# Products of the identity in the planned gaps of the matmul engine, a branch whose idle side follows in line, and a new order, in a planned four-stage block

## The chip, the cores and the metric

The kernel runs on one core of a Trainium2 chip. The metric is the device time of one execution in microseconds (us): the median of several runs. One further execution was taken with the hardware profiler; its span runs from the first to the last instruction.

## What is computed

The input `x` is 32 sequences of 256 tokens with 128 channels, float32. Four residual steps follow one another, each behind a layer normalisation:

```python
x = x + attn_a(layernorm(x), ...)   # delta-rule recurrence over 256 steps, 128 x 128 state, gated
x = x + ffn(layernorm(x), w_gate, w_up, w_down)    # silu(x @ wg.T) * (x @ wu.T) @ wd.T, hidden 384
x = x + attn_b(layernorm(x), ...)   # in-projection, causal convolution of 4 taps, silu,
                                    # state-space scan in chunks (4 heads of 64), gate, norm, out-projection
x = x + ffn(layernorm(x), w_gate, w_up, w_down)    # the same weights again
```

The recurrence of `attn_a` is, per token, `S = S @ (a * (I - b * k k^T)) + b * v k^T` and `o = (q @ S) * gate`. The weights of `ffn` come as integers in -127..127 and are scaled by 1/127.

## The kernel before

**Tiling.** Two sequences make a unit: 512 tokens, four tiles of 128. There are 16 units, and `units()` writes down for each, in turn, `attention` (stage 0), `ffn` (stage 1), `ssd` (stage 2) and `ffn` (stage 3), with a load of `x` ahead and a store of the result behind. In `attention` the recurrence is a blocked triangular inverse: VectorE inverts blocks of 16 by forward substitution (tiles `rows_a`, `u_a`, `step_a`), after their elements went through DRAM (`blocks_a`), and the matmul engine doubles the blocks from 16 to 128 (`pt_a`, `p_a`, with copies `t_a` on ScalarE between, and `pair` for the last level). In `ffn` the products are `fg`, `fu` and `fy`; in `ssd` they are `pz`, `pc` (the convolution's input, read by VectorE into `cy_s`), `pl`, `cb_ps`, `sy_ps`, `pf`, `gT_ps` and `so`. `norm_t` makes the transposed normalised input, `xT_ps`, for every stage.

**The planner.** None of the helpers (`matmul`, `transpose`, `act`, `vec`, `pool`, `dma`) emits anything: each adds an `Op` with an engine, a cost in ns (`busy`), a latency (`late`) and its predecessors, worked out from the parts of buffers that it reads and writes. Matmuls are recorded at line 238, transposes at 251, ScalarE at 259 and 261, VectorE at 275, GpSimd at 292, DMAs at 302, whatever they compute. `Planner.run` then makes a list schedule of all operations of all units over PE, DVE, ACT, POOL and SP: at each step it takes, of the operations that could start within 20 ns of the earliest on their engine, the one with the lowest key. The key is `at(unit)`, that is a multiple of `period` plus a `SHIFT` for each unit (with the last three units drawn together by `LAST`), plus the length of the unit's remaining path, plus a `STAGE` for each of the four stages. It is raised by `SWITCH` for an activation function whose table is not loaded, and by `KEEP` for a change between full products and 64-column pieces (`op.cut`, the `sy_ps` pieces). The plan's start times sort the operations, and in that order they are emitted; each engine executes its own in order. The plan's times themselves are used for nothing else.

**Buffers.** Every buffer takes one of a fixed number of slots of its kind (`SLOTS`); kind `ps` is the eight PSUM banks. A bank is claimed when its first product is placed, no earlier than `EARLY` ns ahead of the time at which everything that the bank's products need from outside (`gate`) is done. An operation on the chip waits for its operands and, where it is the first to write a slot, for the last reader of the buffer that had the slot before it.

**The branch.** A product of the float32 pair form (`exact`) serves where the weights are small integers. At line 1203 every engine loads the flag `large`; at line 1204 a `tc.If(large > 0)` holds a second program of the whole computation with full weights, planned and emitted anew. With these inputs the flag is 0, and every engine jumps over it to the kernel's end.

Constants that the change touches are at lines 153 to 166, `add` at 203, `gates` at 312, `run` from 333, the identity `ident` at 509, the branch at 1204.

Of the kernel before, what the change touches and what calls it, by code (L numbers as in the profile page):

```python
# [18 lines left out]
P = 128  # L19
# [128 lines left out]
class Planner:  # L148
# [2 lines left out]


    SLOTS = {"ps": 8, "m": 56, "l": 10, "t": 12, "s": 64, "d": 6, "g": 6, "b": 3, "e": 4}
    SWITCH = 76800.0
    HOP, SLACK = 30.0, 130.0
    STAGE = (0.0, -8900.0, 1900.0, 0.0)
    EARLY = 0.0
    SPARE = {"ps": 0.5, "m": 3, "l": 0.5, "t": 1, "s": 2, "d": 0.5, "g": 0.5, "b": 0.5, "e": 0.5}
    LAST = 0.12
    SHIFT = (18900.0, -4200.0, 0.0, 0.0, 1500.0, 11400.0, 1600.0, 1500.0, 0.0, 0.0, 19300.0, -27800.0, -1400.0, -9200.0, -7200.0, -5400.0)  # L160
    HALF = "be"
    RATE = 270.0
    LANES = 8
    CUT = 150.0
    KEEP = 3900.0
    SIZES = {"ps": 512, "m": 512, "l": 1024, "t": 64, "s": 32, "d": 512, "g": 8192, "b": 384, "e": 12288}

    def __init__(self, tc, pools, period, window):
# [34 lines left out]
    def add(self, eng, busy, late, emit, outs, ins, table=None, after=(), lock=False):  # L203
        op = Op()
        op.eng, op.busy, op.late, op.emit, op.table, op.lock = eng, busy, late, emit, table, lock
        op.unit, op.n, op.stage = self.unit, len(self.ops), self.stage
        op.preds, op.succs, op.bufs = {p.n: p for p in after}, [], []
        op.moves, op.cut, op.batch = 0.0, 0, ()
        for v, write in [(v, False) for v in ins] + [(v, True) for v in outs]:
            if not isinstance(v, View):  # L210
                continue
            bits = v.bits()
            for other, obits, lanes, owrite in v.buf.seen:
                if (
                    other is not op and (write or owrite) and bits & obits
                    and lanes[0] < v.lanes[1] and v.lanes[0] < lanes[1]
                ):
                    op.preds[other.n] = other
            kept = v.buf.kind == "c" and not v.buf.again
            assert self.setup or not (kept and write)  # L220
            if self.setup or not kept:
                v.buf.seen.append((op, bits, v.lanes, write))
            if v.buf.kind == "c" and v.buf.tile is None:
                v.buf.tile = self.pools["c"].tile(list(v.buf.dims), v.buf.dtype, tag=v.buf.name, name=v.buf.name)
            if v.buf.kind != "c" and v.buf not in op.bufs:
                op.bufs.append(v.buf)
        for p in op.preds.values():
            p.succs.append(op)
        self.ops.append(op)
        return op  # L230
# [42 lines left out]
    def vec(self, name, out, *args, ins=(), more=0, n=None, rate=0.96, **kw):  # L273
        def emit():
            getattr(self.tc.nc.vector, name)(real(out), *map(real, args), **{k: real(v) for k, v in kw.items()})  # L275

        busy = (_count(out) if n is None else n) / rate + 65 + more

        data = {"tensor_tensor": 2, "tensor_tensor_scan": 2, "scalar_tensor_tensor": 3, "tensor_scalar": 1}.get(name, 0)
        data = [v for i, v in enumerate(args[:data]) if (name, i) != ("scalar_tensor_tensor", 1)]  # L280
        lock = bool(data) and not any(isinstance(v, View) and v.buf.kind == "ps" for v in data)
        self.add("DVE", busy, 85, emit, [out], list(args) + list(kw.values()) + list(ins), lock=lock)

    def pool(self, name, out, *args, ins=(), cost=None, **kw):
        n = _count(out)
        if cost is None:
            cost = {
                "tensor_tensor": 1.66 * n + 149, "tensor_scalar": n + 260, "tensor_copy": n + 190, "memset": 0.97 * n + 60,
            }.get(name, n / 2 + 100)

        def emit():
            getattr(self.tc.nc.gpsimd, name)(real(out), *map(real, args), **{k: real(v) for k, v in kw.items()})  # L292

        lock = name == "tensor_tensor" and n > NT
        self.add("POOL", cost, 40, emit, [out], list(args) + list(kw.values()) + list(ins), lock=lock)
# [16 lines left out]
    def gates(self):  # L312
# [7 lines left out]
        for b, ops in users.items():  # L320
# [4 lines left out]
                    of.add(self.ops[n])  # L325
            b.gate = {p for op in ops for p in op.preds.values()} - of

    def at(self, unit):

        late = max(0, unit - (self.units - 3))  # L330
        return (unit - late + late * self.LAST) * self.period + self.SHIFT[unit]

    def run(self):
# [9 lines left out]
        for op in ops:  # L343
            op.key = (self.at(op.unit) + longest[op.unit] - op.tail + self.STAGE[op.stage], op.n)
            op.wait, op.ready, op.placed = len(op.preds), 0.0, False
# [6 lines left out]
        free = dict.fromkeys(engines, 0.0)  # L352
# [9 lines left out]
        order = []  # L362
        while len(order) < len(ops):
            best = None
            for e in engines:
                rest = []
                for op in cands[e] if e != "PE" or not rest_of else rest_of:
# [6 lines left out]
                    for b in op.bufs:  # L374
                        if b.slot is None:
# [5 lines left out]
                            if b.kind == "ps":  # L381
                                if not all(p.placed for p in b.gate):
                                    ok = False
                                    break
                                t = max([t] + [p.done - self.EARLY for p in b.gate])
                    if ok:
# [5 lines left out]
                if e == "ACT" and table is not None:  # L392
                    same = [
                        ((k[0] + (self.SWITCH if op.table and table not in op.table else 0), k[1]), t, op)
                        for k, t, op in same
                    ]
                if e == "PE":
                    same = [((k[0] + (self.KEEP if op.cut != cut else 0), k[1]), t, op) for k, t, op in same]
                pick = min(same, key=lambda x: x[0])
# [3 lines left out]
            t, op = best  # L403
# [35 lines left out]
                oldest += 1  # L439
        self.span = max(op.done for op in ops)  # L440
        order.sort(key=lambda op: (op.start, op.n))
        with self.tc.manual_schedule():
            for op in order:
                for b in op.bufs:
                    if b.tile is None:
                        size = self.SIZES[b.kind]
                        flat = self.pools[b.kind].tile([1 if b.kind in "dge" else P, size], BF16 if b.kind in self.HALF else F32, tag=f"{b.kind}{b.slot[1]}", name=b.name + self.mark)
                        b.tile = flat[:, : b.size]
                        if len(b.dims) > 2:
                            names = " ".join(f"d{i}" for i in range(1, len(b.dims)))  # L450
                            b.tile = b.tile.rearrange(
                                f"p ({names}) -> p {names}", **{f"d{i}": b.dims[i] for i in range(2, len(b.dims))}
                            )
                op.emit()


# [5 lines left out]
def hybrid_block(ctx: ExitStack, tc: tile.TileContext, ins: dict, out: bass.AP):  # L462
# [36 lines left out]
    pl = Planner(tc, pools, period=17900.0, window=6)  # L499
# [6 lines left out]
            pattern=pattern, channel_multiplier=by,  # L506
        )

    ident = pl.const([P, P], "ident")
    pool("memset", ident, 0.0)  # L510
    select(ident, ALU.not_equal, 0, [[-1, P]], 1, fill=1.0)

# [124 lines left out]
    def whole(name, src):  # L637
        wi = pl.buf("m", [P, NF, P], f"wi_{name}").bitcast(I32)
        pl.dma(wi, src, late=3600)
        wf = pl.buf("m", [P, NF, P], f"wf_{name}")  # L640
        vec("tensor_copy", wf, wi)
        return wf

    def turned(name, wf):
        pt = pl.buf("ps", [P, NF, P], f"wt_{name}")
        for f in range(NF):
            pl.transpose(pt[:, f, :], wf[:, f, :], ident)
        return pt
# [15 lines left out]
    large = pl.const([P, 1], "large", I32)  # L664
# [516 lines left out]
    def units():  # L1181
        pl.setup = False
        for g in range(n_units):
            pl.unit = g
            rows_of = slice(g * SEQS, (g + 1) * SEQS)
            x0 = big([P, NT, P], f"x0_{g}")
            pl.dma(x0, x_in[rows_of].rearrange("s (c p) d -> p (s c) d", p=P))
            pl.stage = 0
            x1 = attention(g, x0)
            pl.stage = 1  # L1190
            x2 = ffn(g, x1, "f", "x2")
            pl.stage = 2
            x3 = ssd(g, x2)
            pl.stage = 3
            x4 = ffn(g, x3, "h", "x4")
            pl.dma(out[rows_of].rearrange("s (c p) d -> p (s c) d", p=P), x4)
        pl.run()
# [3 lines left out]


    large = nc.values_load(large.real()[0:1, 0:1], min_val=0, max_val=P)
    with tc.If(large > 0):
        exact, (w_gate, w_up) = False, full
        pl.restart()
        pl.mark = "_full"
        for name, dst, src in (("gate_full", w_gate, gate_src), ("up_full", w_up, up_src)):
            vec("tensor_copy", dst, turned(name, whole(name, src)))
        units()  # L1210
# [34 lines left out]
```

## Time and profile before

| | us |
|---|---|
| median of 3 runs | 805.45 |
| lowest and highest | 802.44, 805.91 |
| the profiled execution | 806.73 |
| its span | 804.9 |
| PE busy, instructions | 744.7, 5485 |
| DVE busy, instructions | 684.3, 2386 |
| ACT busy, instructions | 597.2, 1443 |
| POOL busy, instructions | 364.0, 597 |
| mean granted clock of TensorE | 0.975 |

PE is the matmul engine (TensorE), PEld its weight loads, DVE VectorE, ACT ScalarE, POOL GpSimd, SP SyncE. The busy time of PE includes each product's way through the array, so that neighbours overlap and a busy PE is not a full one. `PEclk` and "granted clock" are the share of TensorE's full clock that the chip grants. A float32 product is two records in the trace. The names of tiles are those of the program with the unit's number left out, so `p_a` stands for all products of that name in `attention`. A wait is named after what ended last before it, which can be an operand or the last reader of a buffer's previous content.

### The profile page before, as it was taken

Reading aid. Unit: us, or ns where it says so; the run is one execution under the profiler, and the core shown is the slowest. Engines: PE = TensorE matmul, PEld = TensorE weight load, DVE = VectorE, ACT = ScalarE, POOL = GpSimd, SP = SyncE. Lnnn points to the kernel's source line nnn. Section 1 sums busy time; section 2 is a strip of 40 time slices with the busy share of each in tenths; the row PEclk is TensorE's granted clock in tenths of the full one; section 3 lists DMA queues with packets and bytes.
Section 4 is the critical chain, followed back from the end, with each engine's and each line's share of the span. In section 5 each row is a group of like instructions: output and inputs, shape, how many; then the busy total and the mean of one; then the engine's idle time right before and its main releaser. Section 6 shows DMA issues by size and latency. Waiting matters only on the chain.

```text
span 804.9 us, 16786 instructions
## 1 busy us (share of the span) xinstructions
PE 744.7 (93%) x5485; PEld 616.5 (77%) x5485; DVE 684.3 (85%) x2386; ACT 597.2 (74%) x1443; POOL 364.0 (45%) x597
## 2 busy tenths in 40 slices
PE   5958999899999999999999999899999999998886
PEld 4646886687878888877988878686789988776775
DVE  4794799989988889889999689989898778999964
ACT  5833467979687877779787798897955578997862
POOL 8994332262452815514732634646631123243550
PEclk9976999999999999999999999999999999999999
DMA  5221110010110002101011002011201000000001
GB/s 145 82 68 42 29 42 1 5 33 1 56 30 24 22 7 67 42 27 33 18 30 31 27 15 58 16 45 44 67 4 43 14 5 1 5 15 5 13 10 44
DMA packets 42159, 25.48 MB, mean 32 GB/s; under 512 B 18448, under 2 KB 37840, under 8 KB 42064
## 3 DMA queue, kind: packets, MB, share of 16 engines
q1 hardware_dynamic: 41056, 24.13, 11.1%
q8 instruction: 45, 0.74, 0.4%
q14 instruction: 50, 0.41, 0.2%
q10 hardware_dynamic: 1008, 0.20, 0.1%
HBM read 19.16 MB, written 5.14 MB: 30 GB/s over the span
## 4 chain that ended last, share of the span: by engine, by line
PE 52%; DVE 20%; ACT 15%; POOL 5%; issue 3%; DMA 2%; SPq 1%; ACTq 0%; DVEq 0%; POOLq 0%
PE p_a L238 6%; PE fy_f L238 5%; DVE cy_s L275 4%; PE fy_h L238 4%; PE fg_f L238 3%; ACT L261 3%; PE sy_ps_s L238 3%; PE so_s L238 2%; PE fu_f L238 2%; PE pc_s L238 2%; PE fg_h L238 2%; PE fu_h L238 2%; PE pt_a L251 2%; DVE u_a L275 2%; PE cb_ps_s L238 2%
## 5 line engine op out<-in xcount | busy, mean ns | idle before, releaser
L275 DVE SCALAR_TENSOR_TENSOR cy_s<-pc_s,cw,cy_s 128x510 f32<-128x510 f32 (+2 forms) x192 | 137.6, 731 | 2.9 <-ACT cy_s L261 2.3
L261 ACT ACT_TABLE_LOAD x66 | 84.7, 1283 | 9.9 <-DMA x<-in_L_attn_a_x_dram 5.8
L238 PE MATMUL fy_f<-wdT,hT_f 128*128 128x128 f32 x384 | 74.5, 280 | 0.0
L238 PE MATMUL fy_h<-wdT,hT_h 128*128 128x128 f32 x384 | 72.1, 281 | 0.6 <-DVE hT_h L275 0.3
L238 PEld LDWEIGHTS fy_f<-wdT,hT_f 128*128 128x128 f32 x384 | 61.4, 191 | 6.3 <-issue 3.6
L238 PE MATMUL pc_s<-xT_s,w_xbc 128*128 128x512 f32 x128 | 64.5, 599 | 1.3 <-ACT gT_s L259 0.7
L238 PEld LDWEIGHTS fy_h<-wdT,hT_h 128*128 128x128 f32 x384 | 59.1, 191 | 8.1 <-issue 4.3
L275 DVE TENSOR_TENSOR step_a<-rows_a,u_a 128x16 f32<-128x16 f32 (+14 forms) x240 | 51.7, 216 | 7.5 <-DMA rows_a<-blocks_a 3.1
L275 DVE TENSOR_TENSOR u_a<-u_a,step_a 128x16 f32<-128x16 f32 (+14 forms) x240 | 54.3, 227 | 3.9
L261 ACT ACTIVATE cy_s<-pc_s,cb,cw 128x512 f32<-128x512 f32 x64 | 48.3, 779 | 9.3 <-PE pc_s L238 9.1
L292 POOL TENSOR_TENSOR xd_s<-xt_s,dt_s 128x512 f32<-128x512 f32 x32 | 33.2, 1045 | 42.9 <-ACT xt_s L259 42.2
L238 PE MATMUL so_s<-w_out,gT_s 128*128 128x128 f32 x256 | 45.8, 290 | 1.9 <-DVE cy_s L275 1.2
L238 PEld LDWEIGHTS so_s<-w_out,gT_s 128*128 128x128 f32 x256 | 39.7, 204 | 6.6 <-ACT cy_s L261 1.4
L261 ACT ACTIVATE sc_s<-cy_s 128x512 f32<-128x512 f32 x64 | 38.9, 636 | 3.6 <-DVE cy_s L275 1.9
L275 DVE SCALAR_TENSOR_TENSOR sm_s<-pl_s,cb_s 128x512 f32<-128x512 f32 x64 | 41.3, 680 | 0.3 <-ACT pl_s L261 0.2
L292 POOL TENSOR_TENSOR sy_s<-sy_s,yo_s 128x256 f32<-128x256 f32 x32 | 24.6, 773 | 35.5 <-DVE sy_s L275 14.2
L238 PEld LDWEIGHTS p_a<-t_a,neg_a 128*128 128x128 f32 x256 | 36.4, 203 | 5.5 <-ACT t_a L259 3.7
L238 PE MATMUL p_a<-t_a,neg_a 128*128 128x64 f32 x256 | 38.1, 280 | 1.8 <-DVE x L275 1.3
L238 PEld LDWEIGHTS p_a<-x_a,t_a 128*128 128x128 f32 x256 | 36.6, 201 | 3.7 <-ACT t_a L259 2.3
L238 PE MATMUL p_a<-x_a,t_a 128*128 128x64 f32 x256 | 37.9, 274 | 1.0 <-ACT t_a L259 1.0
L259 ACT COPY t_a<-pt_a 128x256 f32<-128x256 f32 (+1 forms) x64 | 20.2, 316 | 24.0 <-PE pt_a L251 22.9
L275 DVE TENSOR_TENSOR hT_f<-fth_f,fu_f 128x512 f32<-128x512 f32 x48 | 31.2, 681 | 7.3 <-PE fu_f L238 4.8
(253 smaller groups left out, 2420.7 us busy)
## 6 DMA issues: line engine op xcount, KB each, us to landing
rows_a<-blocks_a SPq DMA_DIRECT2D x128, 64.0 KB
x<-in_L_attn_a_x_dram SPq DMA_DIRECT2D x16, 256.0 KB
dec_a<-row_a SPq DMA_DIRECT2D x16, 256.0 KB
out_dram<-x SPq DMA_DIRECT2D x16, 256.0 KB
blocks_a<-neg_a SPq DMA_DIRECT2D x128, 4.0 KB
cuts_s<-cut_s SPq DMA_DIRECT2D x48, 8.0 KB
sums_t<-cuts_s SPq DMA_DIRECT2D x32, 12.0 KB
sums_s<-cuts_s SPq DMA_DIRECT2D x16, 24.0 KB
```

What stands on the lines that cost most here:

```text
L238: self.tc.nc.tensor.matmul(real(out), lhsT=real(lhsT), rhs=real(rhs), start=start, stop=stop)
L251: self.tc.nc.tensor.transpose(real(out), real(in_), real(ident))
L259: self.tc.nc.scalar.copy(real(out), real(in_))
L261: self.tc.nc.scalar.activation(real(out), real(in_), func, bias=real(bias), scale=real(scale), **kw)
L275: getattr(self.tc.nc.vector, name)(real(out), *map(real, args), **{k: real(v) for k, v in kw.items()})
L292: getattr(self.tc.nc.gpsimd, name)(real(out), *map(real, args), **{k: real(v) for k, v in kw.items()})
```

## The change

It has three parts. A new method `keep_busy` walks the plan's PE operations in order of start and looks at the gap between the end of one and the start of the next (`free` begins at 1700 ns). If the gap is over `IDLE` (300 ns), if no PE operation has yet written the bank's buffer and if the operation is not a 64-column piece, it notes `int(gap * 0.7 / 223)` fillers. These are emitted just ahead of the operation: products of the identity with itself, 128 columns, float32, into the first columns of the operation's own bank, which the operation then overwrites. Nothing reads them, and the plan is made without them.

The branch gets `preferred_fallthrough_block=False`, which asks that the side not taken by `large > 0` follow in line.

Seven numbers of the planner are changed, which give a new order of all operations on all engines.

```diff
-    SWITCH = 76800.0
+    SWITCH = 46100.0
     HOP, SLACK = 30.0, 130.0
-    STAGE = (0.0, -8900.0, 1900.0, 0.0)
-    EARLY = 0.0
+    STAGE = (0.0, -7600.0, 1900.0, 0.0)
+    EARLY = 300.0
...
-    LAST = 0.12
-    SHIFT = (18900.0, -4200.0, 0.0, 0.0, 1500.0, 11400.0, 1600.0, 1500.0, 0.0, 0.0, 19300.0, -27800.0, -1400.0, -9200.0, -7200.0, -5400.0)
+    LAST = 0.1
+    SHIFT = (18900.0, -4200.0, 0.0, 0.0, 1500.0, 11400.0, 1600.0, 1500.0, 0.0, 0.0, 6700.0, -27800.0, -1400.0, -9200.0, -7200.0, -6000.0)
...
-    KEEP = 3900.0
+    IDLE, WARM = 300.0, 0.7
+    KEEP = 3100.0
...
+    def keep_busy(self, order):
+
+
+        written, free = set(), 1700.0
+        for op in order:
+            if op.eng != "PE":
+                continue
+            bank = next(b for b in op.bufs if b.kind == "ps")
+            gap = op.start - free
+            if gap > self.IDLE and bank not in written and not op.cut:
+                op.warm, op.bank = int(gap * self.WARM / 223), bank
+            written.add(bank)
+            free = op.start + op.busy
...
         order.sort(key=lambda op: (op.start, op.n))
+        self.keep_busy(order)
...
+                for _ in range(op.warm):
+                    n = min(P, op.bank.size)
+                    one = self.ident.real()
+                    self.tc.nc.tensor.matmul(op.bank.flat[:, :n], lhsT=one, rhs=one[:, :n], start=True, stop=True)
                 op.emit()
...
-    ident = pl.const([P, P], "ident")
+    ident = pl.ident = pl.const([P, P], "ident")
...
-    with tc.If(large > 0):
+    with tc.If(large > 0, preferred_fallthrough_block=False):
```

## The prediction

> **What bounds the kernel now.** I read the page first, then the matmul engine's clock record and busy time by stage, then the chain of waits inside the slow stages, then the matmul engine's waits, then the last microseconds.
>
> The page:
>
> ```profile
> span 804.9 us, 16786 instructions
> ...
> PE 744.7 (93%) x5485; PEld 616.5 (77%) x5485; DVE 684.3 (85%) x2386; ACT 597.2 (74%) x1443; POOL 364.0 (45%) x597
> ...
> PEclk9976999999999999999999999999999999999999
> ...
> PE 52%; DVE 20%; ACT 15%; POOL 5%; issue 3%; DMA 2%; SPq 1%; ACTq 0%; DVEq 0%; POOLq 0%
> ```
>
> The matmul engine (PE) is the nearest to full and holds 52% of the chain. How full it really is comes from the start-to-start times of its records where it runs without a stop: a 128-column float32 product is two records of about 111 ns, a 512-column one two of 430 ns. Pricing every record so gives 677 us of work at full clock. Walking the records in order, each starting when the one before has taken its price, leaves 102 us of real gaps, 60 us of them in 69 gaps longer than 0.3 us; the remaining 20 us to the last product (798.5 us) is work at half clock. So there are three pots: 677 fixed, 102 of gaps, 20 of cold clock.
>
> The clock record has 0.5 in 47.90-58.14, 64.96-78.62, 242.46-245.87, 730.56-733.98, 754.46-757.87, 771.52-774.94 and from 802.24 on. Before 17.18 us it has no entry, and the "1.00" that windows print there is empty: two 512-column products take 2.05 us at 12.7 us and 1.02 us at 21.2 us, so the start is cold too. By stage (length, then busy time of PE, PEld, DVE, ACT, POOL, granted clock, DMA):
>
> ```profile
> 42.00:54.00 12.00, 3.57 (x15) 1.97 (x14) 11.15 (x37) 4.38 (x10) 11.59 (x21) 0.75 0.38 111
> ...
> 59.00:65.00 6.00, 4.13 (x21) 2.49 (x19) 5.79 (x24) 2.52 (x12) 1.22 (x7) 1.00 0.02 2
> 65.00:79.00 14.00, 12.70 (x58) 11.67 (x58) 4.12 (x16) 3.68 (x11) 8.53 (x11) 0.51 0.22 59
> ...
> 140.00:700.00 560.00, 540.41 (x4135) 454.28 (x4135) 497.02 (x1734) 443.36 (x1054) 237.28 (x372) 1.00 0.10 28
> ```
>
> From 42 to 54 VectorE and GpSimd are full and PE idles; from 65 to 79 only PE is full, and at half clock. The chain there (start, us), against the same products later at full clock:
>
> ```profile
> 64.96 1.98 PE p_a L238 x8
> ...
> 67.39 1.99 PE p_a L238 x8
> ...
> 69.95 1.11 PE pt_a L251 x4
> 71.06 0.64 PE kT_ps_a L251 x3
> 71.70 1.86 PE p_a L238 x8
> ...
> 74.01 1.97 PE p_a L238 x8
> 75.98 1.71 PE pt_a L251 x8
> 77.69 1.58 PE p_a L238 x10
> ```
>
> ```profile
> 102.69 0.84 PE p_a L238 x8
> ...
> 113.72 0.22 PE fy_f L238 x2
> ```
>
> Eight p_a records cost 1.98 us cold and 0.84 us warm. Last, line 1204, the branch:
>
> ```profile
> L1204 SPq EVENT_SEMAPHORE  x8: 17/17/17, 803.0 to 803.5; - x8
> ...
> L1204 SPq COMPARE_BRANCH  x1: 53/53/53, 799.8 to 799.8; - x1
> ```
>
> SyncE branches at 799.85 and executes its next instruction at 802.98: 3.1 us of nothing. The last output bytes land at 801.81.
>
> **What the Trainium skill says.** "TensorE: Matmul & The Clock Gate", section "What's actually happening": the array's clock is cut to half by default and after an idle window, given back after a busy one, in windows of 3413 ns. The trace agrees on the steps: four cold entries are 3.41 us, the others 10.24 and 13.65, three and four of them. The same page, "HAM oscillation": gaps over about 3.4 us recool it. Here the trace is stricter: from 65 to 79 gaps of 0.4 to 0.7 us kept it cold for four windows, and it warmed after solid work (75.8 to 78.6). "Runtime: NRT & Kernel Launch", "Instruction fetch mechanics": a taken branch out of the fetched pages waits for a fetch by DMA; the 3.1 us after the branch, with two instruction packets of 0.42 to 1.29 us inside, fit. "ScalarE: Activation LUTs", "What ACT_TABLE_LOAD costs": 1283 ns a load; the page shows 66 with mean 1283.
>
> **The change part by part**, against the profiled execution's own 806.73 us (span 804.9 and 1.83 around it); it lies 1.28 above the median of the three runs, 805.45, and I carry that over.
>
> *The branch.* If the side with no work follows in line, SyncE goes on at 799.95: its eight semaphore steps (0.6 us) lie beside the last output's landing at 801.81, after which its waits (up to 0.46 us) and the closing 0.78 us remain: end at about 803.1 for 804.9. VectorE's own jump (799.35 to 802.27) goes as well. -1.7; at least 0 (layout unchanged), no more than that, since the landing takes its place.
>
> *Fillers: what they are.* One is a 128-column product of two records, 0.22 us warm, 0.43 cold. Their number depends on the gaps of the plan, which the profile doesn't show; the nearest row is the trace's own gaps. The rule int(gap x 0.7 / 223), put on the 69 gaps, gives 60 before 66 us (13.4 us), 70 from 66 to 700 (15.6 us), 27 after (6.0 us), some 157 at most; gaps before a product that is not its bank's first write, or that is a 64-column piece, get none.
>
> *Fillers: cold clock.* The stage 65-79: PE pieces on the chain sum to 12.2 us up to 78.62, at half clock, so 6.1 us are to be had. They need the idle of 42-54 and of 61-65 filled, and these are waits for GpSimd, DMA and VectorE, which the planner prices. I take -5. The idle of 42-54 itself and the cold work of 50-58 lie under VectorE's u_a, step_a and e_a: 0. At the start, cold PE pieces of 0.48, 0.85, 1.12, 0.56, 1.92 and 1.76 us lie on the chain between 9.4 and 16.6 (6.7 us, so 3 at most), but GpSimd carries the chain from 17 to 37 and has only some 1.6 us idle between 14 and 18: -1. At 771.5-774.9 about 3.3 us of the chain are cold: 1.6 at most, -1. The three other cold windows lie under VectorE (2.0 of 2 us at 730 and 754), or last 3.4 us: -0.5. Sum -7.5, bounds -11 and 0.
>
> *Fillers: their own cost.* A filler writes the bank of the product behind it, so it cannot start before that bank's last reader. Where the operand is late, it is hidden; where the bank is, filler and product both run afterwards, and each filler costs 0.22 us on PE with everything behind it. The matmul engine's waits show both (total, times, longest):
>
> ```profile
> PE pf_s L238 <- POOL xe_s L292: 2.6, 2, 1.8
> ...
> PE xT_ps_f L251 <- DVE cy_s L275: 1.9, 2, 1.2
> ```
>
> xe_s is pf_s's operand; cy_s is no operand of xT_ps_f but a reader of a bank. Of the fillers counted after 66 us, 36 (8.0 us) stand in gaps that an operand ends, 61 (13.6 us) in others. I take a third of the 13.6, since many of these gaps stand inside a bank already begun or ahead of an engine that isn't needed soon: +4.5, bounds 0 and +14.
>
> *The new order.* SWITCH, STAGE, KEEP, LAST, EARLY and two SHIFTs reorder every engine's queue. What it can move is the gaps: those over 0.3 us from 66 to 700 hold about 29 us. EARLY 300 lets a bank be claimed up to 0.3 us ahead of its last operand, so that PE is at the spot when it comes; against it, a lower SWITCH can add table loads (a tenth of 66 is 7 x 1.283 = 9 us on an engine with 207 us idle) and a claimed bank is lost to others. I take a tenth of the 29: -3, bounds -11 and +9. The number of loads, DMAs and float operations elsewhere I leave.
>
> Sum: 806.73 - 1.7 - 7.5 + 4.5 - 3.0 = 799.0; less 1.28: 797.8, forecast 798.
>
> **The rivals.** (1) *Slower: the bank wait.* Fillers stand mostly where PSUM banks, not operands, are late. For it: the 61 against 36 above, with eight banks for four stages in flight. Against: a third of these gaps can have no filler. With 13.6 us exposed and cold gains of 4 the sum is 806.73 - 1.7 - 4 + 13.6 - 1.3 = 813, 810 with the order's -3. It decides once more than some 11 us of filler (50 pieces) runs while its product could have. (2) *The cold stretch was covered.* VectorE (11.15 of 12 us in 42-54) and GpSimd set the ramp, a warm PE waits for them, and only the branch is gained, with some filler cost: 803 to 806. Against it: VectorE is busy 4.12 of 14 us from 65 to 79. (3) *The order pays most.* A third of the 29 us of gaps goes instead of a tenth: 798 - 7 = 791. (4) *The fillers do nothing for the clock*, being too thin at 0.7 of a gap; this ends with (2).
>
> **How the numbers follow.** Forecast 0.45 (792 to 804), rival 1 0.20, rivals 2 and 4 0.15, rival 3 0.20. One half per cent, about what this measurement can tell from no change, is 4 us: faster is under 801.4, slower over 809.5. Faster: four fifths of 0.45, all of rival 3, a fifth of rival 2: 0.59. Slower: most of rival 1 and the order's upper bound: 0.21. Same: 0.20. The range leaves out a tenth on either side: 786 to 811.
>
> **What would show it.** The clock record should hold full clock from about 8 us through 79, with p_a x8 near 0.84 us at the ramp, and the work that now ends at 79 should stand some 5 us earlier; SyncE's first step after the branch should come within 0.2 us of it, and the tail after the last output's issue shrink by 1.7 us; filler records (ident as both operands) should number 70 to 160. Wrong it is if the stage 140-700 has more PE work and as much gap, or if the waits of fillers name readers of banks; also if table loads rise well past 66, or if the ramp ends at the same time with a warm clock.

## The result, and the profile after

The changed kernel takes 816.16 us (median of 6 runs, 812.19 to 817.19), the kernel before, in the same runs, 804.27 us (802.07 to 805.91): a ratio of 1.0138, 95% interval 1.0107 to 1.0168. It is slower by 12 us, outside the predicted range of 792 to 804.

The lines of its page that answer to those shown of before:

```profile
span 814.8 us, 17321 instructions
...
PE 765.7 (94%) x5751; PEld 643.1 (79%) x5751; DVE 685.4 (84%) x2386; ACT 596.6 (73%) x1441; POOL 364.3 (45%) x597
...
PEclk9988999999999999998999999999999999998998
...
PE 49%; DVE 20%; ACT 15%; POOL 6%; issue 4%; SPq 3%; DMA 2%; DVEq 0%; ACTq 0%; POOLq 0%
```

PE has 266 more records, that is 133 fillers, and the other engines do what they did, but for two table loads fewer on ScalarE (64 for 66). The same walk through the matmul records as in the prediction (each priced by its start-to-start time at full clock, the rest counted as gap or as stretching by a cold clock) gives:

| us | before | after |
|---|---|---|
| work of the products, at full clock | 676.7 | 676.7 |
| fillers, at full clock | 0 | 29.6 |
| gaps, the first wait included | 101.9 | 86.0 |
| stretching by the cold clock | 19.9 | 14.0 |
| end of the last product | 798.5 | 806.3 |
| from the start of the last VectorE operation to the end | 6.2 | 8.3 |

So with 29.6 us of fillers the gaps are only 15.9 us less and the cold clock 5.9 less, and the end itself grew by 2.1. The same walk through the new order without fillers (the first experiment below) gives 106 us of gaps and 23 of stretching: set against that order, the fillers took away about as much time as they needed, and no more.

The stages of the ramp (columns as before: length, busy PE, PEld, DVE, ACT, POOL, granted clock, DMA):

```profile
42.00:54.00 12.00, 9.93 (x68) 8.11 (x67) 9.71 (x34) 4.79 (x16) 10.78 (x17) 1.00 0.20 51
...
59.00:65.00 6.00, 6.00 (x24) 5.16 (x24) 4.08 (x16) 1.82 (x10) 2.31 (x7) 0.50 0.05 11
65.00:79.00 14.00, 13.88 (x99) 11.86 (x98) 11.68 (x41) 6.89 (x22) 7.68 (x11) 0.97 0.06 20
140.00:700.00 560.00, 541.26 (x4175) 458.97 (x4176) 486.65 (x1706) 432.65 (x1033) 240.11 (x375) 0.99 0.11 27
```

In 42-54 PE is now busy and warm, in 65-79 it is at full clock, with 99 records where there were 58, and the chain there shows the product at its warm price:

```profile
66.97 0.84 PE p_a L239 x8
...
68.78 0.85 PE p_a L239 x8
```

From 55.5 to 65.7 us the clock is still at half (the row 59-65), where the prediction had it full through 79. The work that ended at 79 us now ends at 74, as forecast, and the amount of work that was done at 101.4 us before (some 59 of the 677 us) is done at 94.5 us. Not all of this is the fillers' doing: the new order without fillers has done it at 97.8. By 370 us the lead is still 5.4 us. It is lost between 370 and 430 us (8 us) and between 703 and 760 us (another 9). Nearly all of the loss is the order's too: without a filler it loses 8 and 7 us on the same work. What the fillers add to it is told by the waits of PE on their line, 473 (total, times, longest):

```profile
PE cs_s L473 <- ACT xt_s L260: 3.3, 1, 3.3
PE pl_s L473 <- DVE xr_f L276: 2.6, 1, 2.6
...
PE fu_f L473 <- DVE x L276: 1.7, 1, 1.7
...
PE gT_ps_s L473 <- ACT gT_s L260: 1.4, 1, 1.4
PE pz_s L473 <- ACT zs_s L262: 1.3, 2, 0.7
```

A filler reads the identity and nothing else, and the identity is made in the first microseconds, so what it waits for here can only be the last reader of its bank. The worst place, PE in order of time (start, length, then the idle time before and what ended it):

```profile
731.43 1.04 PE L252 MATMUL xt_ps_s<-ident,sc_s 128*128 128x128 f32 x8
735.76 4.64 PE L473 MATMUL cs_s<-ident 128*128 128x128 f32 x20 [3.29 <-ACT xt_s L260]
740.19 0.64 PE L239 MATMUL cs_s<-le,grid 128*128 128x128 f32 x2
```

PE stood idle for 3.3 us until ScalarE had read the bank, and the clock fell. Then ten fillers ran for 4.4 us at half clock, and the product behind them came last. The gap that they were to fill was over when they could begin. With the order alone PE waits there as well, but the product follows at once:

```profile
737.00 0.49 PE L239 MATMUL cs_s<-le,grid 128*128 128x128 f32 x2 [2.90 <-ACT xt_s L260]
```

The branch, in the changed kernel at line 1224 (the kernel's end is at 1261):

```profile
L1224 SPq EVENT_SEMAPHORE  x8: 17/17/17, 807.8 to 810.8; - x8
...
L1224 SPq COMPARE_BRANCH  x2: 38/48/57, 807.7 to 810.9; - x2
```

```profile
L1261 SPq EVENT_SEMAPHORE  x10: 17/28/28, 813.5 to 814.8; - x10
```

SyncE does go on at once, at 807.8, but its eight steps last until 810.8, since after two of them it waits 2.6 us. This wait is for the landing of the output: the third step waits for the semaphore of the last output's transfer, which rises for the last time at 810.47, and the step follows at 810.49. Then comes what the prediction did not have: a second branch at 810.9, from the end of the block to the end of the kernel, after which the next instruction executes at 813.5, 2.6 us later. In the kernel before, the same landing (802.34) lay inside the stop after the jump; now the stop comes behind the landing.

### The profile page after: what moved, and what is told of

The parts are those of the page before. It is cut to its first block, busy times and chain, and to the rows that moved or that the text cites. A ratio compares the mean times of both kernels' runs of the same rounds, so it can differ in the third digit from the quotient of the medians.

```text
span 814.8 us, 17321 instructions
## 1 busy us (share of the span) xinstructions
PE 765.7 (94%) x5751; PEld 643.1 (79%) x5751; DVE 685.4 (84%) x2386; ACT 596.6 (73%) x1441; POOL 364.3 (45%) x597
## 4 chain that ended last, share of the span: by engine, by line
PE 49%; DVE 20%; ACT 15%; POOL 6%; issue 4%; SPq 3%; DMA 2%; DVEq 0%; ACTq 0%; POOLq 0%
PE p_a L239 5%; PE fy_f L239 4%; DVE cy_s L276 4%; PE fy_h L239 4%; SPq L303 3%; ACT L262 3%; PE sy_ps_s L239 2%; PE fu_f L239 2%; PE pt_a L252 2%; PE fg_f L239 2%; PE fg_h L239 2%; PE pc_s L239 2%; DVE step_a L276 2%; PE fu_h L239 2%; PE so_s L239 2%
## 5 line engine op out<-in xcount | busy, mean ns | idle before, releaser
L276 DVE TENSOR_TENSOR step_a<-rows_a,u_a 128x48 f32<-128x48 f32 (+14 forms) x240 | 53.8, 226 | 8.1 <-DMA blocks_a<-neg_a 2.5
L276 DVE TENSOR_TENSOR u_a<-u_a,step_a 128x8 f32<-128x8 f32 (+14 forms) x240 | 51.3, 216 | 3.2
L293 POOL TENSOR_TENSOR xd_s<-xt_s,dt_s 128x512 f32<-128x512 f32 x32 | 33.2, 1044 | 45.8 <-ACT xt_s L260 38.3
L239 PE MATMUL so_s<-w_out,gT_s 128*128 128x128 f32 x256 | 43.8, 277 | 0.1
L239 PEld LDWEIGHTS so_s<-w_out,gT_s 128*128 128x128 f32 x256 | 38.0, 192 | 2.9 <-ACT gT_s L260 0.5
L276 DVE TENSOR_TENSOR hT_h<-fth_h,fu_h 128x512 f32<-128x512 f32 x48 | 31.9, 678 | 8.0 <-ACT fth_h L262 4.5
L262 ACT ACTIVATE pl_s<-pl_s 128x512 f32<-128x512 f32 x64 | 33.4, 583 | 6.6 <-PE pl_s L239 6.5
L252 PE MATMUL pt_a<-ident,x_a 128*128 128x128 f32 x192 | 34.6, 281 | 2.9 <-DVE x_a L276 1.3
L239 PE MATMUL po_a<-pr_a,k_a 128*128 128x128 f32 x192 | 36.9, 279 | 0.1
```

Source lines behind the costliest of these rows:

```text
L239: self.tc.nc.tensor.matmul(real(out), lhsT=real(lhsT), rhs=real(rhs), start=start, stop=stop)
L252: self.tc.nc.tensor.transpose(real(out), real(in_), real(ident))
L262: self.tc.nc.scalar.activation(real(out), real(in_), func, bias=real(bias), scale=real(scale), **kw)
```

## The experiments

Each is the kernel before or the changed kernel with parts taken out or put in, or with one or two of the planner's numbers changed. None leaves out any of the computation that the output needs. The branch is as before unless it is named. Times are medians; ratios are to the kernel before in runs on the same chip, and can differ by up to 0.2% from the ratio of the medians. Traces are of one execution each.

**Each part alone.** The order alone, against the changed kernel:

```diff
-        self.keep_busy(order)
...
-    with tc.If(large > 0, preferred_fallthrough_block=False):
+    with tc.If(large > 0):
```

> The kernel before with only the seven planner numbers of the change: no fillers, the branch as before. Theory A (the fillers cost it: they stand behind late banks and use 30 us of the matmul engine): the order is neutral, 801 to 807 us beside 804 for the kernel before. Theory B (the order costs it): 810 us or more, near the changed kernel's 816.

Measured 811.08 us, ratio 1.0061 (1.0043 to 1.0080). The order costs about 5 us by itself, so theory A does not hold; theory B's 810 is reached, but the time is not near the changed kernel's 816.

The fillers alone, against the changed kernel (the other four numbers are put back in the same way):

```diff
-    SHIFT = (18900.0, -4200.0, 0.0, 0.0, 1500.0, 11400.0, 1600.0, 1500.0, 0.0, 0.0, 6700.0, -27800.0, -1400.0, -9200.0, -7200.0, -6000.0)
+    SHIFT = (18900.0, -4200.0, 0.0, 0.0, 1500.0, 11400.0, 1600.0, 1500.0, 0.0, 0.0, 19300.0, -27800.0, -1400.0, -9200.0, -7200.0, -5400.0)
...
-    EARLY = 300.0
+    EARLY = 0.0
...
-    with tc.If(large > 0, preferred_fallthrough_block=False):
+    with tc.If(large > 0):
```

> The kernel before with only the fillers: order and branch as before. The plan holds 114 of them (25 us). Theory A: 808 to 814 us, the ramp to about 80 us some 5 us earlier, the rest later. Theory B: 796 to 802, since the clock gain of the ramp stays and the fillers are hidden.

Measured 809.14 us, ratio 1.0050 (1.0029 to 1.0071). The fillers cost as well, as theory A says, and neither theory holds alone. In its trace the work that took 101.4 us before takes 98.1, and the ramp is not warm throughout:

```profile
61.70 0.67 PE L239 MATMUL pvq_a<-xT_a,gT_a 128*128 128x256 f32 x2 [2.87 <-DVE neg_a L276]
62.79 0.27 PE L252 MATMUL pd_a<-ident,ab_a 128*4 128x128 f32 x1 [0.41 <-DVE u_a L276]
62.90 0.60 PE L239 MATMUL pvq_a<-xT_a,gT_a 128*128 128x256 f32 x2
64.04 1.97 PE L239 MATMUL p_a<-t_a,neg_a 128*128 128x64 f32 x8 [0.55 <-ACT t_a L260]
65.80 0.74 PE L473 MATMUL p_a<-ident 128*128 128x128 f32 x2
66.47 1.97 PE L239 MATMUL p_a<-x_a,t_a 128*128 128x64 f32 x8
```

The idle 2.87 us at 59-62 has no filler, because the plan has no such gap there. The clock falls at 63.5 all the same, and two p_a groups of 1.97 us are cold until 70.3, where before it was four, until 78.6. Whether the 3.3 us are the fillers' gain cannot be told from this: four traces of this order without a filler in the ramp (the kernel before, the branch alone, and the two runs below with late fillers only) take 101.4, 100.7, 98.2 and 103.3 us for the same work.

The branch alone, against the kernel before:

```diff
-    with tc.If(large > 0):
+    with tc.If(large > 0, preferred_fallthrough_block=False):
```

> The kernel before with only the fall-through of the branch. From the changed kernel's last microseconds (8.3 us from the start of the last VectorE operation to the end, for 6.2 before): +2.1 us, 806 to 807. The rival, the prediction's own step: -1.7, 802 to 803.

Measured 808.15 us, ratio 1.0038 (1.0013 to 1.0064). From the start of the last VectorE operation to the end it takes 9.06 us, in the kernel before 6.20. SyncE's lines in that run (line 1223 is its branch):

```profile
L1223 SPq EVENT_SEMAPHORE  x8: 17/17/17, 796.9 to 800.5; - x8
...
L1223 SPq COMPARE_BRANCH  x2: 43/48/53, 796.8 to 800.6; - x2
```

SyncE again waits twice: 3.15 us among the steps, until the landing (the semaphore rises last at 800.16, the step follows at 800.17), and 2.82 after the second branch. The second branch comes 4.90 us after the start of the last VectorE operation, which is when the kernel before, with its one stop of 3.13 us and its steps behind it, is already at line 1241. So the loss is the stop after the second branch.

Order and fillers together, against the changed kernel:

```diff
-    with tc.If(large > 0, preferred_fallthrough_block=False):
+    with tc.If(large > 0):
```

> The changed kernel with the branch as before: order and fillers. If the branch costs 2.1 us and the parts add: 814 us, 2 below the changed kernel's 816. If the branch saves 1.7: 818.

Measured 811.17 us, ratio 1.0072 (1.0052 to 1.0093), below the changed kernel's 1.0138, so the branch costs here too. It is 5 us where 2 were expected, but the two ratios stem from different chips and their intervals are 0.4 to 0.6% wide. Beside the order alone (1.0061) the fillers cost only 0.1% on this order, not clear of nothing. The parts alone sum to 1.5%, the change measured 1.4%.

**Which fillers cost.** From here to the bank-free ones, against the run with the fillers alone. Those whose product the plan starts before 66 us:

```diff
-            if gap > self.IDLE and bank not in written and not op.cut:
+            if gap > self.IDLE and bank not in written and not op.cut and op.start < 66000:
```

> The kernel before with only those fillers that the plan starts before 66 us: 58 of the 114. Theory (the ramp's fillers gain some 3 us through the clock and lie beside other engines' work; the later ones cost): 800 to 803 us, ratio 0.994 to 0.998. Rival (the ramp is held by VectorE and GpSimd, its gain is lost again by 100 us): 804 to 806, ratio 1.000.

Measured 801.83 us, ratio 0.9978 (0.9952 to 1.0004): on the side of a gain, not clear of none. The three traces of the old order with the ramp's fillers take 98.1, 98.2 and, in this run, 103.1 us for the work that took 101.4 before, so single traces do not settle it either. This run's profiled execution, one of its slower ones (806.21 us), was cold from 62.1 to 86.0 us in spite of the fillers.

Those from 66 us on:

```diff
-            if gap > self.IDLE and bank not in written and not op.cut:
+            if gap > self.IDLE and bank not in written and not op.cut and op.start >= 66000:
```

> The kernel before with only the fillers that the plan starts at 66 us or later: 56 of the 114 (12.5 us at full clock). Theory (they stand behind late banks and are paid): 809 to 813 us, ratio 1.006 to 1.010, and the two halves add up to the ratio with all fillers, 1.005. Rival (the loss is the early fillers' own time): 804 to 806.

Measured 807.35 us, ratio 1.0034 (1.0014 to 1.0054): the later ones are paid, though less than the theory's 1.006 to 1.010. The halves sum to 0.1%, all of them measured 0.5%; the widths of the three intervals allow no more than that the late ones are the loss.

What they wait for can be counted in each trace: of the time of a group of fillers, that part is exposed which lies after the moment at which the product behind it had all its semaphores. In the run with the late ones it is 8.6 of 16.0 us, in the run with all 7.7 of 17.1 late (from 66 us of the trace on) and 1.0 of 18.2 in the ramp; with the new order 14.6 of 23.9 late, and in the changed kernel 15.5 of 24.7 late and 2.7 of 21.4 in the ramp. On the new order more fillers stand behind late banks.

Fillers only for that part of a gap in which the plan has the bank free:

```diff
-            gap = op.start - free
+            gap = op.start - max(free, bank.slot[0])
```

> The kernel before with fillers in all planned gaps, but each gap counted only from the time at which the plan has the bank free: 74 fillers, 58 of the ramp as in the last but one, and 16 later. Theory (a filler costs only where its bank is late): 801 to 804 us, ratio 0.995 to 0.999, about as with the ramp's alone. Rival (every late filler costs its 0.22 us, whatever it waits for): 3.5 us above the ramp's alone.

Measured 808.17 us, ratio 1.0034 (1.0000 to 1.0069), against the expectation. The trace does what the theory says. What PE and its weight loads waited for at the fillers' line with the late fillers, and with this rule (total, times; a wait of both counts twice):

```profile
  DVE cy_s L276: 6.6, 6
  ACT gT_s L260: 4.8, 4
  ACT cb_s L260: 4.7, 2
```

```profile
  POOL ident L293: 3.3, 2
  DVE cy_s L276: 0.3, 1
```

The waits for readers of banks are gone but for 0.3 us, and from 66 us of the trace on 0.9 us of 7.8 is exposed. Yet the interval leaves out the theory's 0.995 to 0.999 and holds the rival's 1.002. The ten executions lie far apart, between 800.85 and 811.54 us: three of them had a mean clock of 0.985 or more, of the run with the ramp's fillers eight of twelve, and what decides this is not shown. The 16 late ones of them alone:

```diff
-            gap = op.start - free
-            if gap > self.IDLE and bank not in written and not op.cut:
+            gap = op.start - max(free, bank.slot[0])
+            if gap > self.IDLE and bank not in written and not op.cut and op.start >= 66000:
```

> The kernel before with only the 16 fillers after 66 us whose gap the plan counts from the time the bank is free. In the trace of the run with these and the ramp's, some 0.9 us of their time stood before products that were already able to run. Theory (a filler costs only its exposed time): 804 to 806 us, ratio 0.999 to 1.002. Rival (each costs its 0.22 us): 808, ratio 1.004.

Measured 807.31 us, ratio 1.0022 (0.9992 to 1.0052), exposed 0.75 of 5.0 us. This interval holds both answers. Shown is that the late fillers cost, that the bank is what they waited for, and that the rule takes the exposed time away; that the time then comes back is not shown.

**The order.** The plan's own length is 754.0 us for the kernel before and 753.6 for the change. Other orders, without fillers. The first is the kernel before with the SHIFT of unit 12 (counted from 0) raised:

```diff
-    SHIFT = (18900.0, -4200.0, 0.0, 0.0, 1500.0, 11400.0, 1600.0, 1500.0, 0.0, 0.0, 19300.0, -27800.0, -1400.0, -9200.0, -7200.0, -5400.0)
+    SHIFT = (18900.0, -4200.0, 0.0, 0.0, 1500.0, 11400.0, 1600.0, 1500.0, 0.0, 0.0, 19300.0, -27800.0, -400.0, -9200.0, -7200.0, -5400.0)
```

> The kernel before with one other number, SHIFT of unit 12 at -400 for -1400; no fillers, the branch as before. The planner's own length for it is 753.7 us, for the kernel before 754.0, for the order of the change 753.6. Theory A (the plan's length does not tell the time to within 1%; orders of one length scatter): anywhere from 800 to 813 us, so more than 0.4% from the kernel before. Theory B (orders of equal plan length are equal in time, and the change's order has a fault of its own): 803 to 806.

Measured 805.73 us, ratio 0.9995 (0.9975 to 1.0016), as theory B has it.

The run with the order alone, with the SHIFT of unit 0 raised:

```diff
-    SHIFT = (18900.0, -4200.0, 0.0, 0.0, 1500.0, 11400.0, 1600.0, 1500.0, 0.0, 0.0, 6700.0, -27800.0, -1400.0, -9200.0, -7200.0, -6000.0)
+    SHIFT = (21900.0, -4200.0, 0.0, 0.0, 1500.0, 11400.0, 1600.0, 1500.0, 0.0, 0.0, 6700.0, -27800.0, -1400.0, -9200.0, -7200.0, -6000.0)
```

> The order of the change (EARLY 300, no fillers, branch as before) with one more number moved, SHIFT of unit 0 at 21900 for 18900: the planner's own length falls to 748.8 us, 5.2 below the kernel before. Theory A (the plan's length carries over to the chip): 798 to 801 us. Theory C (banks claimed ahead of their operands make the plan shorter than the chip can follow, by some 5 us): 803 to 808. Theory D (the order of the change is only a bad draw; plans scatter on the chip by 1%): no statement on this one alone, 795 to 810.

Measured 804.97 us, ratio 1.0003 (0.9976 to 1.0029), as theory C has it: the plan is 5 us shorter than that of the kernel before, the time is not.

The same, with the SHIFT of unit 5 lowered instead:

```diff
-    SHIFT = (18900.0, -4200.0, 0.0, 0.0, 1500.0, 11400.0, 1600.0, 1500.0, 0.0, 0.0, 6700.0, -27800.0, -1400.0, -9200.0, -7200.0, -6000.0)
+    SHIFT = (18900.0, -4200.0, 0.0, 0.0, 1500.0, 10400.0, 1600.0, 1500.0, 0.0, 0.0, 6700.0, -27800.0, -1400.0, -9200.0, -7200.0, -6000.0)
```

> Another order with EARLY 300 (SHIFT of unit 5 at 10400 for 11400 on top of the change's numbers; no fillers, branch as before), whose planned length, 754.5 us, is that of the kernel before (754.0) and of the change's order (753.6). Theory C: slow as the change's order, 808 to 813 us. Theory D: as likely near 804 as near 811.

Measured 811.16 us, ratio 1.0078 (1.0047 to 1.0108), again as theory C has it.

The kernel before, with the SHIFT of unit 0 lowered:

```diff
-    SHIFT = (18900.0, -4200.0, 0.0, 0.0, 1500.0, 11400.0, 1600.0, 1500.0, 0.0, 0.0, 19300.0, -27800.0, -1400.0, -9200.0, -7200.0, -5400.0)
+    SHIFT = (18400.0, -4200.0, 0.0, 0.0, 1500.0, 11400.0, 1600.0, 1500.0, 0.0, 0.0, 19300.0, -27800.0, -1400.0, -9200.0, -7200.0, -5400.0)
```

> The kernel before (EARLY 0) with SHIFT of unit 0 at 18400 for 18900, which changes the order from the start; planned length 755.0 us. Theory C: 804 to 807 us, as the other order with EARLY 0 of 753.7 planned, which took 0.9995 of the kernel before. Theory D: more than 0.4% off to either side.

Measured 805.93 us, ratio 1.0008 (0.9989 to 1.0026), and again theory C. So far each order with EARLY 0 took its planned length plus 50 us, each with EARLY 300 its length plus 56. Three runs put this to the test. The order alone with twice the EARLY, and the SHIFT of unit 11 raised, which brings the plan back to the same length:

```diff
-    EARLY = 300.0
+    EARLY = 600.0
...
-    SHIFT = (18900.0, -4200.0, 0.0, 0.0, 1500.0, 11400.0, 1600.0, 1500.0, 0.0, 0.0, 6700.0, -27800.0, -1400.0, -9200.0, -7200.0, -6000.0)
+    SHIFT = (18900.0, -4200.0, 0.0, 0.0, 1500.0, 11400.0, 1600.0, 1500.0, 0.0, 0.0, 6700.0, -26800.0, -1400.0, -9200.0, -7200.0, -6000.0)
```

> An order with EARLY 600 (SHIFT of unit 11 at -26800 on top of the change's other numbers; no fillers, branch as before) of planned length 753.6 us, the same as the change's own. Theory C with a dose (each 300 ns of claiming ahead hides some 6 us from the plan): 753.6 + 62 = 815 us, ratio 1.013. A fixed step from EARLY 0 to any other value: 753.6 + 56 = 810, ratio 1.006. Chance: near 804.

Measured 811.75 us, ratio 1.0082 (1.0061 to 1.0103): nearer to the fixed step than to the dose. The order alone without EARLY:

```diff
-    EARLY = 300.0
+    EARLY = 0.0
```

> The change's order with EARLY back at 0 and the other six numbers as the change has them (no fillers, branch as before); planned length 769.7 us. If the time is planned length plus 50 with EARLY 0: 820 us, ratio 1.019. If the plan's length says nothing at this distance: anywhere from 805 to 815.

Measured 827.01 us, ratio 1.0280 (1.0235 to 1.0324), with five executions from 820.0 to 828.5: plus 57, not 50. The high surcharge is there without EARLY, so theory C falls. The kernel before with EARLY alone:

```diff
-    EARLY = 0.0
+    EARLY = 300.0
```

> The kernel before with EARLY 300 alone; planned length 764.9 us. Planned length plus 56: 821 us, ratio 1.020. If EARLY has no cost beyond the plan (plus 50): 815, ratio 1.013.

Measured 819.63 us, ratio 1.0183 (1.0138 to 1.0227), with four executions: plus 54, between the two. All orders, each put on 804.5 us by its ratio (a surcharge is uncertain by 2 to 4 us):

| order | planned | time | surcharge |
|---|---|---|---|
| before | 754.0 | 804.5 | 50.5 |
| before, SHIFT of unit 12 | 753.7 | 804.1 | 50.4 |
| before, SHIFT of unit 0 | 755.0 | 805.1 | 50.1 |
| before, EARLY 300 | 764.9 | 819.2 | 54.3 |
| change | 753.6 | 809.4 | 55.8 |
| change, SHIFT of unit 0 | 748.8 | 804.7 | 55.9 |
| change, SHIFT of unit 5 | 754.5 | 810.8 | 56.3 |
| change, SHIFT of unit 11, EARLY 600 | 753.6 | 811.1 | 57.5 |
| change, EARLY 0 | 769.7 | 827.0 | 57.3 |

The plan's length does carry over (the order planned 4.8 us shorter than the change's took 4.7 us less, with some 2 us of uncertainty on either), but with a surcharge that is 50 us for the kernel before and orders near it, and 54 to 58 for the rest. SWITCH is no part of it: with 46100 or 76800 and all else equal the plan has the same length and the same gaps. Why the numbers of the kernel before have the low surcharge stays open.

Where the surcharge arises can be seen by setting each PE operation's time on the chip against its time in the plan. In the trace of the order alone the lag grows from 31.4 to 39.0 us between 369 and 442 us, in the kernel before from 31.2 to 33.2 over the same work; that is 5.6 of the 7.2 us by which the two lags differ at the end. PE in order of time there, order alone:

```profile
370.78 0.78 PE L239 MATMUL p_a<-t_a,neg_a 128*128 128x64 f32 x6
374.15 0.58 PE L239 MATMUL pl_s<-sums_t,sums_s 93*128 93x512 bf16 x1 [2.59 <-DVE xr_f L276]
375.81 0.77 PE L239 MATMUL fg_f<-xT_f,wgT 128*128 128x512 f32 x1 [1.07 <-DVE f_s L276]
```

The stage with these waits, first with the order alone, then in the kernel before:

```profile
367.00:380.00 13.00, 9.29 (x33) 5.90 (x31) 11.79 (x28) 10.57 (x19) 5.68 (x9) 0.74 0.19 48
```

```profile
367.00:380.00 13.00, 11.87 (x61) 8.03 (x60) 12.55 (x36) 12.83 (x26) 7.27 (x12) 1.00 0.20 46
```

Neither product reads what its wait is named after, so both wait for banks. VectorE is busy for most of the time, and then come 6.8 us at half clock, which no plan knows. All four traces of this order, with fillers or without, have such a cold stretch of 6.8 us, from between 370.6 and 373.0 us on; no trace of the old order has one there. The changed kernel waits the same 2.6 us there, with fillers behind the wait: they run after it and do not keep the clock.

**A version that is faster.** The ramp's fillers on the change's order, against the run with order and fillers:

```diff
-            if gap > self.IDLE and bank not in written and not op.cut:
+            if gap > self.IDLE and bank not in written and not op.cut and op.start < 66000:
```

> The change's own order with only the fillers before 66 us (55 of its 133), branch as before. Theory (its 78 later fillers stand exposed for 14.6 us and undo the ramp's gain): 806 to 809 us, below the order alone and the order with all fillers (both 811). Rival (later fillers cost nothing here): 811.

Measured 807.89 us, ratio 1.0030 (1.0014 to 1.0046), below the order alone (1.0061) and the order with all fillers (1.0072), as the theory has it. The late fillers thus cost 0.4% on this order, for 0.3% on the old one.

The same on the order of 748.8 us, against the run before it:

```diff
-    SHIFT = (18900.0, -4200.0, 0.0, 0.0, 1500.0, 11400.0, 1600.0, 1500.0, 0.0, 0.0, 6700.0, -27800.0, -1400.0, -9200.0, -7200.0, -6000.0)
+    SHIFT = (21900.0, -4200.0, 0.0, 0.0, 1500.0, 11400.0, 1600.0, 1500.0, 0.0, 0.0, 6700.0, -27800.0, -1400.0, -9200.0, -7200.0, -6000.0)
```

> The order of planned length 748.8 us (EARLY 300), with only the fillers that the plan starts before 66 us, and the branch as before. If the ramp's fillers gain 2 to 4 us through the clock on any order: 800 to 803 us, ratio 0.995 to 0.998, below both kernels. If their gain was chance: 805.

Measured 799.85 us, ratio 0.9931 (0.9906 to 0.9956), below both kernels. Its page:

```profile
span 797.9 us, 17000 instructions
...
PE 744.9 (93%) x5593; PEld 622.1 (78%) x5593; DVE 684.7 (86%) x2386; ACT 594.9 (75%) x1441; POOL 359.9 (45%) x597
```

It has 54 fillers, of whose 21.0 us 1.0 was exposed. Beside the same orders without fillers, the ramp's fillers measured gains of 0.2, 0.3 and 0.7%; the last two are clear of nothing when the intervals of the two ratios are put together, the first is not.

## Why the prediction was wrong, step by step

The sum was 7.7 us below the profiled execution (-1.7 -7.5 +4.5 -3.0). The parts alone measured, in the same order, +3.1 (0.38%), +4.0 (0.50%) for both steps of the fillers together, and +4.9 (0.61%): 12.0 in all, for 11.9 of the medians.

- *What bounds the kernel*: right. PE's work is 677 us, and what moved the time were its gaps, its clock and its fillers, and the end. (The "two 512-column products" of 2.05 us are the two records of one product; the comparison stands.)
- *The branch, -1.7*: wrong in sign. The step was "SyncE goes on at 799.95: its eight semaphore steps (0.6 us) lie beside the last output's landing". That much is so: SyncE goes on at once and meets the landing among its steps. What the step left out is the end of the block, a branch of its own with a stop of 2.6 to 2.8 us, as long as the one that was to go. The old stop lay beside the landing and cost little, the new one lies behind it and costs all. The gain to be had was also smaller: the landing's semaphore rose last at 802.34, not at 801.81, which left about 0.7 us. The instruction packets of 0.42 and 1.29 us, taken as a sign of a fetch, start inside the stop but end after SyncE had gone on at 802.98, so what fills such a stop is not shown. The bound "at least 0" rested on a layout that no trace of before showed.
- *Cold clock, -7.5*: the mechanism is right, the size perhaps. The fillers alone bring the recorded cold time from 35 us to 19 us (medians of the executions); by the rate given below that is an estimated 5.5 us. The ramp's fillers, measured whole, gained 1.8, 2.5 and 5.8 us on three orders. The -5 of the stage 65-79 was to come from filled idle in 42-54 and 61-65; the first was filled, the second lies in no planned gap.
- *The fillers' own cost, +4.5*: the mechanism is right, and the term is mis-sized. The number of fillers was met (133, for 70 to 160), and the sign named for being wrong, waits of fillers for readers of banks, is there. But 4.5 us were taken as exposed, and it was 7.7 of the 17.1 us of late fillers on the old order, and 15.5 of 24.7 in the changed kernel. Late gaps are for the most part waits for the bank already in the plan: counting each gap only from the time at which the plan has the bank free takes away 40 of the 56 late fillers of the old order, and none of the ramp's 58. Both fillers' steps together were to give -3.0; they measured +4.0 on the old order and about +1 on the new one, where the ramp's gain pays for nearly all of it.
- *The new order, -3*: wrong in sign, and the largest miss. The step was "I take a tenth of the 29", a direction without a ground. The two plans differ by 0.4 us, so the plan promised nothing; on the chip the order alone has 4 us more of gaps than the kernel before (106 for 102, the first wait included) and 3 us more of stretching by the cold clock, much of it in a few places. Why the chip takes 5 us longer for this plan than for one of the same length stays open.
- *Rival 1* named the mechanism that decides for the late fillers, and its point: "more than some 11 us of filler ... runs while its product could have". It was 18.2 us. That its 813 is near the measured 816 is in part luck: it has the branch at -1.7 where it cost 3.1, and no term for the order, which cost 4.9.

## What to carry to other kernels

Work that fills an idle engine must be free to run in that idle time: ask what the filler itself waits for. Here that was, in the later part, the bank of the product which it was to stand in for, and such fillers cost 0.3 and 0.4%; where the bank was free, in the ramp, they gained 0.3 and 0.7% on two orders. A stop that lies beside a transfer's landing costs little, and moving work out of it gains little; ask what comes after the landing. Two orders of equal planned length can differ on the chip by 5 us and more, so test the order apart from everything that comes with it. And one trace of a stage is one draw: the same 59 us of work, in the same order and without fillers, took 98 to 103 us in four traces.

## What the runs showed of the hardware that was not expected

The first branch of a conditional block whose idle side follows in line cost SyncE 0.1 us; the branch at the end of that block cost a stop of 2.6 and 2.8 us, where the jump over the block had cost one of 3.1.

The clock fell after idle times much shorter than its own shortest cold entries, 3.41 us: in the trace of the kernel before it fell at 242.46 us, with one gap of 1.1 us and one of 0.2 in the 3.4 us ahead, and at 64.96, with gaps of 0.9, 0.4 and 0.5.

Within one kernel the time follows the recorded cold time: over all kernels a microsecond at half clock goes with 0.35 us of time, and with the ramp's fillers on the old order the eight executions at a mean clock of 0.985 to 0.988 took 800.2 to 802.0 us, the four at 0.977 to 0.980 took 805.7 to 808.4. This goes together; which of the two brings the other is not shown. With this spread, the intervals of the ratios here are 0.3 to 0.9% wide.

The start of an execution is cold although the record has no entry there: with fillers from 1.7 us on, the first entry of full clock stands at 7.7 us for 17.2 before.
